# A burst of attention beside a projection: sums over keys first, scores behind them; and sums of exponentials ahead of a subtraction

## The chip, the cores and the metric

The kernel runs on one core of a Trainium2 chip. The metric is the device time of one execution in microseconds. The engines run at the same time and meet through semaphores: TensorE (PE in the profile) multiplies matrices into PSUM, VectorE (DVE) and ScalarE (ACT) work elementwise, GpSimd (POOL) helps with casts, and SyncE (SP) issues most DMAs. PEld is the loading of TensorE's weights.

## The reference

Eight images of 512 channels by 32x32 pixels (1024 tokens) go through two attention layers, in float32.

Layer 0, per image: group norm (32 groups); `qkv = qkv_w @ h + qkv_b`, split into 8 heads of 64 channels; q, k and v are quantized to 256 levels, each with one scale and zero point over the whole tensor; per head `w = softmax(q^T k / sqrt(64))` and `a = w v`; then `x = x + proj_w @ a + proj_b`.

Layer 1, per image: group norm; q, k, v by 512x512 weights; one head of 512 channels: `softmax(q k^T / sqrt(512)) v`; a last 512x512 projection; `x + proj`.

## The kernel before

The quantizer's range needs q, k and v of all images, so a first phase computes these and stores them to DRAM. The second phase takes them up again. Layer 0's attention of the next image runs beside layer 1 of the current one, on the same TensorE, interleaved by Python generators.

**Attention of layer 0** (`attention`, L825). A unit is one pair of heads (j), one half of the 1024 queries (hf) and one block of 128 keys (s), for both heads. A unit's steps:

- `scores`: four st matmuls per two units (64 rows of keys by 512 queries, bf16) into a PSUM tile of two banks. Then ACT takes the exponential into a float32 tile pt. `scores` draws its PSUM tile by `pair_ps` from the pool `ps_s`, which has two buffers (L730).
- `split`: pt is cast to a float16 tile (ACT, or GpSimd for every fourth unit), and VectorE subtracts the cast from pt, so that the two float16 parts carry the value. The pair of parts is the tile two; there are six (L740), and four of pt (L739).
- `over_keys`: av matmuls, the exponentials' parts times v, summed over keys in one PSUM bank.
- `totals`: sm matmuls, the sums of the exponentials over keys, for the division, in another bank.

The loop at L964 makes a burst out of four units: it asks for scores six and eight units ahead, and sums units u to u+3. A burst has two forms: with `dense`, two pairs of units, each av then sm, with the second scores between them; otherwise av of all four, sm of all four, then the second scores. In both, the first scores (units u+6 and u+7) stand at the head of the burst.

**The projection of layer 0** (`project`, L1026). For each half of the tokens and each of four blocks of output channels, four matmuls make one PSUM tile pj of 512 columns (the profile has two rows for each float32 matmul, so 8 of pj for a tile); VectorE evicts it, adding bias and x, and stores it, and takes statistics for layer 1's norm (BN_STATS and an aggregate). Between the two halves it yields, and the attention of the image after gets a burst there. For image 0 the projection's tiles come from the pool `ps_o`. For images 1 to 7 the call at L1482 hands over `score_bank`, so that pj tiles come from the same two buffers of `ps_s` as the scores.

**Layer 1** (`layer1`, L1380). The products are made in seven multiplications instead of eight (`seven`, L1123), with sums of quarters formed on VectorE beforehand. In `o_run` (L1270), exponentials times v, the sums of quarters of the exponentials are t1, t2, t3 and t4. They are made by deferred VectorE operations named "p" to "p4" (L1461 to L1469); "p2" is t2 = p22 - t1. Another deferred kind, "acc" (L1432), adds up the exponentials for the softmax's row sums. Between products 4 and 5 of the second half stands the projection of the next image, with a burst ahead of it, one between its halves, and one behind it (`first`, at L1481 to L1485).

**What sets the order.** Instructions of TensorE, VectorE and ACT run in the order in which the Python program issues them. For VectorE and ACT that order is planned: `InOrder` (L67) keeps a clock for each engine. `later` files an operation with a cost, a time from which it may run and a due time; `fill` picks, up to a limit, the one with the earliest possible start, and at equal starts the earliest due. `settle` forces an operation out before its reader. The bursts are driven at L1622: each yield of the layer's generator advances the attention by one burst, and a negative yield sets `dense` for it.

Of the kernel before, what the change touches and what calls it, by code (L numbers as in the profile page):

```python
# [53 lines left out]
def attn_pair_kernel(  # L54
# [12 lines left out]
    class InOrder:  # L67
# [66 lines left out]
        def settle(self, what):  # L134

            while True:
                i = next((i for i, c in enumerate(self.chores) if c[0] == what), None)
                if i is None:
                    return
                self.begin(i)  # L140

    dve, act, pe = InOrder(nc.vector), InOrder(nc.scalar), InOrder(nc.tensor)
# [137 lines left out]
    with ExitStack() as fast:  # L280
# [544 lines left out]
        def attention():  # L825
# [64 lines left out]
            def over_keys(us):  # L890
                need(us[-1])
                awaits(ready[us[-1]])
                pe.t += 0.12
                for u in us:
                    b, j, hf, s = units[u]
                    if s == 0:
                        avs[b, j, hf] = av_bank(f"av_{b}_{j}_{hf}")
                    for w in range(2):
                        for i, r in enumerate(HALF):
                            mm(  # L900
                                avs[b, j, hf][r, :], lhsT=pairs[b, j][2][:, s, r],
                                rhs=parts[u][:, w, i, :], start=(s == 0 and w == 0),
                                stop=(s == NT - 1 and w == 1),
                            )
# [59 lines left out]
            for u in range(0, len(units), 4):  # L964
                b, j, hf, s = units[u]
                if hf == 0 and s == 0:
                    n = b * PAIRS + j + 1
                    if n < B * PAIRS:
                        pairs[divmod(n, PAIRS)] = load_pair(*divmod(n, PAIRS))
                    settle("qv")  # L970

                def two(what, v):
                    if v < len(units):
                        what(v)
                        what(v + 1)

                pe.t += 0.12  # L980
                two(scores, u + 6)
                if dense:
                    over_keys((u, u + 1))
                    totals((u, u + 1))
                    two(split, u + 6)
                    two(scores, u + 8)
                    over_keys((u + 2, u + 3))
                    totals((u + 2, u + 3))
                else:
                    over_keys(range(u, u + 4))  # L990
                    totals(range(u, u + 4))
                    two(split, u + 6)
                    two(scores, u + 8)
                if s == NT - 4:
                    finish(b, j, hf)
                two(split, u + 8)
                pe.t += 0.15
                last = (j, hf, s) == (PAIRS - 1, NH - 1, NT - 4)
                yield 6.0 + (hf == NH - 1 and s == NT - 4), b + last
# [26 lines left out]
        def project(b, bank=bank):  # L1026

            settle("ao")  # L1030
            st, mvs[b] = stat_tiles(CC, f"b{b}")
            wp0 = wps.pop(b)
            for hf in range(NH):
                for oc in range(CC):
                    ps = bank(f"pj_{b}_{hf}_{oc}")
                    for cc in range(CC):
                        mm(
                            ps, lhsT=wp0[:, cc, bass.ts(oc, P)], rhs=ao[b, cc][:, hf, :],
                            start=(cc == 0), stop=(cc == CC - 1),
                        )  # L1040
                    xx = xts[b][:, oc, bass.ts(hf, 512)]

                    def evict():
                        dve.scalar_tensor_tensor(
                            xx, ps, vec[:, V_PB0 + oc : V_PB0 + oc + 1], xx, ALU.add, ALU.add
                        )
                        nc.sync.dma_start(x1_d[b][oc // 2][hf][:, oc % 2, :], xx)

                    def stats(oc=oc, hf=hf, xx=xx):
                        dve.bn_stats(st[:, oc, hf, :], xx)  # L1050
                        if hf == NH - 1:
                            aggregate(mvs[b], st, oc)

                    dve.do(elements(550), evict)
                    dve.later("pj", 0.62 + 0.2 * hf, stats, within=4.0)
                    chore()
                if hf + 1 < NH:
                    yield -1
            settle("pj")
            for k in [k for k in ao if k[0] == b]:  # L1060
                del ao[k]
# [318 lines left out]
        def layer1(b, steps):  # L1380
# [36 lines left out]
            for hf in range(NH):  # L1417
                last = hf == NH - 1
                if last:
                    gq = yield from a_run(1)  # L1420
                rx = {}
                for row, col in ((0, 0), (1, 1), (1, 0)):
                    load_x1(b, hf, row, col, rx)
                acc = l1p.tile([P, 512], F32, tag="acc1", name=f"acc1_{b}_{hf}")
                pts, rows = {}, []

                def gather(pt, row, acc=acc, rows=rows):
                    for i in range(2):
                        rows.append(pt[:, 2 * row + i, :])
                        if len(rows) > 1:  # L1430
                            two = rows[0] if len(rows) == 2 else acc, rows[-1]
                            dve.later(  # L1432
                                "acc", elements(512), lambda two=two: tt(acc, *two, ALU.add), act.t,
                                7.0,
                            )


                ps_ = [
                    gq[:, i : i + 2].rearrange("p s k n -> p (s k) n") for i in (0, 2, 4)
                ]  # L1440
                t1, t2, t4 = ps_
                for ns in alike:
                    yield from run(
                        *(s_block(b, hf, n, gq, pts, gather) for n in ns),
                        at=3 + 2 * hf - ns[0],
                    )
                    if ns[0] == 0:
                        (p11, p12) = (pts[0][:, :, c * 256 : (c + 1) * 256] for c in range(2))
                        dve.later(
                            "p", elements(1024),  # L1450
                            lambda t1=t1, p11=p11, p12=p12: tt(t1, p12, p11, ALU.subtract),
                            act.t, 12.0,
                        )
                p21, p22 = (pts[1][:, :, c * 256 : (c + 1) * 256] for c in range(2))
                settle("p")

                def third(p12=p12, p22=p22):
                    settle("acc")
                    tt(p12, p22, p12, ALU.subtract)

                dve.later(  # L1461
                    "p2", elements(1024), lambda t1=t1, t2=t2, p22=p22: tt(t2, p22, t1, ALU.subtract),
                    dve.t, 5.0,
                )
                dve.later("p3", elements(1024), third, act.t, 9.0)
                dve.later(
                    "p4", elements(1024), lambda t4=t4, t2=t2, p21=p21: tt(t4, p21, t2, ALU.subtract),
                    act.t, 14.0,
                )  # L1469
                if last and b + 1 < B:  # L1470
                    load_wp(b + 1, act.dma_start)
                    load_x2(b + 1, act.dma_start)
                if done >= B:
                    load_x1(b, hf, 0, 1, rx, aop)
                settle("v")
                between = [lambda: iter((1,)), lambda: iter(()), lambda: iter(())]
                if b + 1 < B and last:

                    def first():
                        nonlocal ahead  # L1480
                        yield -1  # L1481
                        yield from project(b + 1, score_bank)  # L1482
                        yield 1
                        ahead = norm1(b + 1, score_bank)
                        next(ahead)  # L1485

                    def more():
                        next(ahead)
                        yield from ()

                    between = [first, more, more]
                yield from o_run(b, hf, vt, vs, ps_, pts, acc, rx, between)
# [95 lines left out]
        F_FIRST = 12.0  # L1588
        pos, done = 0.0, 0
        dense = True  # L1590

        def advance():
            nonlocal pos, done
# [26 lines left out]
            e.t = pe.t  # L1620
        InOrder.planned = True
        for n in others():  # L1622
            dense = n < 0
            advance()


# [362 lines left out]
```

## Time and profile before

| | us |
|---|---|
| median of 3 runs | 2689.42 (2688.77 to 2689.55) |
| the profiled execution's own time | 2690.02 |
| its span, first to last instruction | 2688.2 |
| PE busy | 2594.8 |
| DVE busy | 1904.8 |
| ACT busy | 1259.0 |
| POOL busy | 201.7 |

The profiled execution took 1.8 us more than its span, and 0.6 us more than the median run. The first phase, and attention of image 0, last until 787 us, where the projection of image 0 begins. From 1031 us a projection begins every 244.7 to 246.4 us: that is one image of layer 1 with the next image's attention inside. The last image's layer 1 (from 2494 us) has no attention beside it.

A row of the timeline gives the start, the time to the end of the merged instructions, the engine, line, operation and tiles, the count, and in brackets the idle time of the engine before it and what ended it. L81 and L192 are the recording helpers, so rows are told apart by their tiles: st are scores, pt exponentials, two the float16 parts, av and sm the sums over keys, pj the projection, h its evicted output, s, o and g layer 1's products. A row of the waits gives the total, the number and the longest.

### The profile page before, as it was taken

Reading aid. Unit: us, or ns where it says so; the run is one execution under the profiler, and the core shown is the slowest. Engines: PE = TensorE matmul, PEld = TensorE weight load, DVE = VectorE, ACT = ScalarE, POOL = GpSimd, SP = SyncE. Lnnn points to the kernel's source line nnn. Section 1 sums busy time; section 2 is a strip of 40 time slices with the busy share of each in tenths; the row PEclk is TensorE's granted clock in tenths of the full one; section 3 lists DMA queues with packets and bytes.
Section 4 is the critical chain, followed back from the end, with each engine's and each line's share of the span. In section 5 each row is a group of like instructions: output and inputs, shape, how many; then the busy total and the mean of one; then the engine's idle time right before and its main releaser. Section 6 shows DMA issues by size and latency. Waiting matters only on the chain.

```text
span 2688.2 us, 33380 instructions
## 1 busy us (share of the span) xinstructions
PE 2594.8 (97%) x13110; PEld 1657.8 (62%) x13110; DVE 1904.8 (71%) x2749; ACT 1259.0 (47%) x1582; POOL 201.7 (8%) x156
## 2 busy tenths in 40 slices
PE   7999999998779999999999999999999999999998
PEld 3455555553225774776577567757765775677687
DVE  6666666647997776876777687678767776876544
ACT  0011111114875665666476556646664765565021
POOL 0000000000220000100100010001001000100000
PEclk9999999998999999999999999999999999999999
DMA  5323223224421123212322321233133223212311
GB/s 196 113 110 125 101 96 117 94 113 146 134 64 40 56 68 118 95 56 94 111 64 71 107 87 56 79 109 94 56 95 110 64 76 103 87 40 69 112 36 37
DMA packets 147464, 241.97 MB, mean 90 GB/s; under 512 B 26592, under 2 KB 92128, under 8 KB 145760
## 3 DMA queue, kind: packets, MB, share of 16 engines
q1 hardware_dynamic: 116448, 181.50, 20.1%
q10 hardware_dynamic: 30848, 58.23, 6.3%
q8 instruction: 105, 1.72, 0.3%
q14 instruction: 63, 0.52, 0.1%
HBM read 152.86 MB, written 86.28 MB: 89 GB/s over the span
## 4 chain that ended last, share of the span: by engine, by line
PE 78%; DVE 9%; issue 7%; DMA 2%; ACT 2%; POOL 1%; SPq 0%; ACTq 0%; DVEq 0%; POOLq 0%
PE s L192 15%; PE o L192 13%; PE qkps L192 10%; PE pj L192 8%; PE av L192 7%; PE v2ps L192 7%; PE g L192 5%; PE vps L192 5%; PE st L192 4%; PE sm L192 4%; DVE two L81 2%; ACT pt L81 1%; DVE sums L81 1%; DVE x L81 1%; DVE h L81 1%
## 5 line engine op out<-in xcount | busy, mean ns | idle before, releaser
L81 DVE TENSOR_TENSOR two<-pt,two 128x1024 f16<-128x1024 f32 x512 | 618.1, 1225 | 165.9 <-POOL two L873 134.7
L81 ACT ACTIVATE pt<-st,esc 128x1024 f32<-128x1024 f32 x512 | 543.5, 1115 | 371.0 <-PE st L192 348.1
L81 ACT CAST two<-pt 128x1024 f16<-128x1024 f32 x364 | 369.5, 1055 | 7.8 <-ACT p L81 5.1
L873 POOL CAST two<-pt 128x1024 f16<-128x1024 f32 x128 | 177.1, 1384 | 1585.5 <-PE sm L192 1376.4
L81 ACT ACTIVATE u<-qkps,qkb 128x512 f32<-128x512 f32 x84 | 57.7, 687 | 476.5 <-PE qkps L192 472.1
L192 PE MATMUL av<-two,v 128*64 128x512 f16 x2048 | 255.3, 387 | 0.6
L192 PE MATMUL s<-g,h 128*128 128x256 f32 x1024 | 234.2, 381 | 0.0
L192 PE MATMUL pj<-ao,wp 128*128 128x512 f32 x512 | 223.9, 595 | 1.5 <-DVE ao L81 1.5
L192 PEld LDWEIGHTS s<-g,h 128*128 128x128 f32 x1024 | 192.9, 190 | 31.8 <-issue 4.3
L192 PE MATMUL st<-q,k 64*128 64x512 bf16 x1024 | 166.5, 386 | 42.3 <-ACT pt L81 35.6
L192 PEld LDWEIGHTS <-v 128*64 128x64 f16 x2048 | 104.1, 110 | 133.1 <-issue 62.0
L192 PE MATMUL s<-g,sums 128*128 128x256 f32 x768 | 178.4, 381 | 0.2 <-DVE p L81 0.2
L192 PE MATMUL o<-p,v 128*128 128x256 f32 x768 | 175.2, 382 | 0.0
L192 PEld LDWEIGHTS pj<-ao,wp 128*128 128x128 f32 x512 | 96.1, 190 | 123.1 <-issue 112.9
L192 PE MATMUL qkps<-x,wqkv 128*128 128x512 f32 x352 | 163.5, 608 | 1.8 <-DVE x L81 1.8
L192 PEld LDWEIGHTS o<-p,v 128*128 128x128 f32 x768 | 144.3, 190 | 25.6 <-issue 6.9
L192 PEld LDWEIGHTS s<-g,sums 128*128 128x128 f32 x768 | 144.7, 190 | 24.2 <-issue 4.6
L192 PE MATMUL qkps<-sums,wa 128*128 128x512 f32 x336 | 153.3, 592 | 0.0
L192 PE MATMUL sm<-two,ones 128*32 128x512 f16 x2048 | 141.6, 386 | 1.3 <-ACT rs L81 1.3
L192 PEld LDWEIGHTS <-k 64*128 64x128 bf16 x1024 | 36.6, 94 | 165.6 <-issue 163.1
L192 PE MATMUL o<-g,vsum 128*128 128x256 f32 x512 | 125.4, 401 | 11.5 <-DVE g L81 11.5
L192 PE MATMUL g<-h,wa 128*128 128x256 f32 x512 | 122.1, 387 | 2.5 <-DVE h L81 2.5
(193 smaller groups left out, 3504.8 us busy)
## 6 DMA issues: line engine op xcount, KB each, us to landing
rs<-rs_d SPq DMA_DIRECT2D x80, 256.0 KB
x<-in_x_dram SPq DMA_DIRECT2D x32, 512.0 KB
raw<-q_d SPq DMA_DIRECT2D x32, 512.0 KB
raw<-k_d SPq DMA_DIRECT2D x32, 512.0 KB
raw<-v_d SPq DMA_DIRECT2D x32, 512.0 KB
x_d<-h SPq DMA_DIRECT2D x64, 256.0 KB
x<-x_d ACTq DMA_DIRECT2D x64, 256.0 KB
out_dram<-x SPq DMA_DIRECT2D x64, 256.0 KB
```

Source lines behind the costliest of these rows:

```text
L81: ins = op(*args, **kw).ins
L192: ins = nc.tensor.matmul(ps, lhsT=lhsT, rhs=rhs, **kw).ins
L873: copy(two[:, 0], pt)
```

## The change

Three edits. A yield may now be -2 or 2, which sets a flag `late` for its burst (-2 is also negative, so `dense` holds as well, but `late` is asked first). A late burst begins with av of two units, then come the first scores, sm of these units, av and sm of the next two, and the second scores at the end. The yield between the projection's halves becomes -2, and the one behind the projection in `first` becomes 2. The deferred operation "p2" gets another earliest time (ACT's clock instead of VectorE's) and another due time (0.5 instead of 5.0 us).

```diff
@@ attention(), the loop over units
                 pe.t += 0.12
-                two(scores, u + 6)
-                if dense:
+                if not late:
+                    two(scores, u + 6)
+                if late:
+                    over_keys((u, u + 1))
+                    two(scores, u + 6)
+                    totals((u, u + 1))
+                    over_keys((u + 2, u + 3))
+                    totals((u + 2, u + 3))
+                    two(split, u + 6)
+                    two(scores, u + 8)
+                elif dense:
                     over_keys((u, u + 1))
                     totals((u, u + 1))
                     two(split, u + 6)
@@ project(), between the halves
                 if hf + 1 < NH:
-                    yield -1
+                    yield -2
@@ layer1(), the deferred t2
                 dve.later(
                     "p2", elements(1024), lambda t1=t1, t2=t2, p22=p22: tt(t2, p22, t1, ALU.subtract),
-                    dve.t, 5.0,
+                    act.t, 0.5,
                 )
@@ layer1(), first()
                         yield from project(b + 1, score_bank)
-                        yield 1
+                        yield 2
                         ahead = norm1(b + 1, score_bank)
@@ the driver
         dense = True
+        late = False
...
         for n in others():
-            dense = n < 0
+            dense, late = n < 0, abs(n) == 2
             advance()
```

## The prediction

> **What bounds the kernel now.** I read the page first: its busy times, its slices and its chain.
>
> ```profile
> span 2688.2 us, 33380 instructions
> PE 2594.8 (97%) x13110; PEld 1657.8 (62%) x13110; DVE 1904.8 (71%) x2749; ACT 1259.0 (47%) x1582; POOL 201.7 (8%) x156
> PE 78%; DVE 9%; issue 7%; DMA 2%; ACT 2%; POOL 1%; SPq 0%; ACTq 0%; DVEq 0%; POOLq 0%
> ```
>
> PE is busy 97% and holds 78% of the chain; every other engine has slack. So a reordering can only gain what PE idles, and it costs whatever PE idles anew. The waits of PE alone, from the first projection that lies beside layer 1 (1031 us) to the end, say how little that is:
>
> ```profile
> PE o L192 <- DVE g L81: 9.6, 5, 1.9
> PE st L192 <- DVE h L81: 6.2, 12, 0.5
> PE st L192 <- ACT pt L81: 1.5, 5, 0.3
> ```
>
> The second line is the one that the change can reach: 12 waits of 0.5 us, two for each of the six projections that take their outputs from the score buffers. Then the timeline of the burst between the halves of one such projection (PE, then ACT), and the head of the burst behind its second half:
>
> ```profile
> 1537.68 0.39 PE L192 MATMUL st<-q,k 64*128 64x512 bf16 x2
> 1538.59 0.39 PE L192 MATMUL st<-q,k 64*128 64x512 bf16 x2 [0.52 <-DVE h L81]
> 1538.91 1.05 PE L192 MATMUL av<-two,v 128*64 128x512 f16 x8
> 1539.90 0.61 PE L192 MATMUL sm<-two,ones 128*32 128x512 f16 x8
> 1540.44 0.61 PE L192 MATMUL st<-q,k 64*128 64x512 bf16 x4
> 1540.98 1.05 PE L192 MATMUL av<-two,v 128*64 128x512 f16 x8
> 1541.96 0.62 PE L192 MATMUL sm<-two,ones 128*32 128x512 f16 x8
> ...
> 1538.11 2.12 ACT L81 ACTIVATE pt<-st,esc 128x1024 f32<-128x1024 f32 x2 [10.46 <-PE st L192]
> 1540.88 2.12 ACT L81 ACTIVATE pt<-st,esc 128x1024 f32<-128x1024 f32 x2 [0.64 <-PE st L192]
> ...
> 1556.44 0.39 PE L192 MATMUL st<-q,k 64*128 64x512 bf16 x2
> 1557.35 0.39 PE L192 MATMUL st<-q,k 64*128 64x512 bf16 x2 [0.52 <-DVE h L81]
> 1557.67 1.92 PE L192 MATMUL av<-two,v 128*64 128x512 f16 x16
> ```
>
> The reader is to see that the second score pair waits for VectorE to evict the last projection tile, that each exponential starts 0.43 to 0.44 us behind its scores, and that 1.53 us of sums (av and sm) stand between the last scores and the next projection tile (1542.51).
>
> Last, stretches of 3.41 us around the long wait of the o products, with the granted clock:
>
> ```profile
> core 0: us, PE busy (x), PEclk, DMA share, GB/s
> 759.15:762.57 3.42, 1.58 (x12) 1.00 0.00 0
> 762.57:765.98 3.41, 2.15 (x16) 0.50 0.00 0
> 1015.15:1018.57 3.42, 1.72 (x8) 1.00 0.74 186
> 1018.57:1021.98 3.41, 3.20 (x15) 1.00 0.01 4
> 1260.91:1264.33 3.42, 1.50 (x7) 1.00 0.35 79
> 1264.33:1267.74 3.41, 3.41 (x10) 0.50 0.00 0
> ```
>
> A stretch with 1.72 us of PE work is followed by full clock, one with 1.58 or less by a stretch at half clock. So idle time of about 1.70 us in a stretch is harmless and 1.83 us halves the next. The stretches keep their own beat: the same wait of 1.9 us halves the clock in images 1, 2, 4 and 5 and not in 0 and 3, where it lies across a boundary. The price shows in the windows from projection to projection: 244.66 us with image 3's, 246.4 us for the others, so 1.7 us.
>
> **The change part by part.** The build's order lists say what moves. ACT, POOL and SP issue the same instructions in the same order, so no DMA is moved. PE runs the same instructions; 13 bursts are reordered: between the halves of projections 0 to 6, and behind projections 1 to 6 (the eighth has no attention left beside it). VectorE has seven swaps beside the projections, and one place where exponential sums move.
>
> *Middle bursts, projections 1 to 6.* Now 1537.68 to 1542.51, 4.83 us. The pieces, start to start: four st matmuls 0.54, eight av 0.985, eight sm 0.55. The new order is av, st, sm, av, sm, st. The first av needs sums that VectorE had ready more than a projection half earlier; the eviction ends 0.86 us behind the burst's start (1538.54), and the second score pair comes at 0.985 + 0.27 = 1.25, so the 0.52 us wait goes. The next scores come at 3.61; the two exponentials before them run 1.42 to 3.54, so that isn't late either. PE's work is 2 x (0.54 + 0.985 + 0.55) = 4.15 us.
>
> But now scores stand last. The projection (score_bank, two buffers) takes its next tile from the buffer that the first of these last scores filled. Its exponential starts at 3.61 + 0.43 = 4.04 and takes 1.11, to 5.15; PE took up work 0.06 us behind an exponential at 805.33. So the projection starts at 5.21: a new wait of 1.06 us, and 0.38 us later than now. Its second tile needs the second exponential (6.16) and comes at 8.6, no wait. Six bursts: +2.3 us. All of PE is queued behind that wait, and VectorE's evictions come 0.38 us later with it. GpSimd's cast of the first pair then starts at the exponential's end (2.53) instead of at the sums' (2.77 now), so it isn't late. ACT ends its exponentials 0.9 us later than now, and the casts behind them; the first subtraction that needs such a cast stands behind an eviction at 8.7, so this is covered by 1.5 us.
>
> *Bursts behind projections 1 to 6.* Now 1556.44 to 1561.04, 4.60 us, av and sm in blocks of 16. New: 4.15 by the same pieces. Behind it come the o products from other buffers, 16 matmuls of 3.7 us, which hide the exponentials; the norm's small matmul, which does use a score buffer, comes after those. Gain 0.45 each, -2.7 us. It reaches the end if the stage behind stays PE's: VectorE finishes the four norm pieces 2.4 us before the g products (1573.55 against 1575.94).
>
> *Middle burst of projection 0.* Its tiles lie in another pool, so nothing waits behind: 802.66 to 807.17 is 4.51, to 4.15: -0.36 us.
>
> *VectorE.* Seven times one subtraction goes behind BN_STATS and the aggregate: 0.69 + 0.21 us later. The eviction behind it still finds all done (the engine idles 0.70 us there), and its reader is a burst more than 10 us on. Cost 0; without cover up to 0.2 us each, since the total is the same. The sums ahead of the subtraction: the lists show it in one place alone, the second half of image 6. Two additions of 0.69 us fill VectorE's 1.29 us idle before 2480.13 and push the subtraction some 0.5 us back, to end near 2481.8; PE reads it at 2486.20. Cost 0; bare, 0.5 us. Everywhere else the wait of 1.9 us before o stays.
>
> *Unseen.* av behind a projection tile, and st behind av, stand nowhere in these bursts; I take the joints at what st behind a projection tile and av behind st cost; between 0 and 0.1 us over 13 bursts, up to +1.3. The shift of all later work by tenths moves the 1.9 us waits against the clock's beat. With -0.36 at image 0 its wait falls whole into a stretch (end 1018.4, boundary 1018.57) and is halved, +1.7; that carries image 1's wait across its boundary, -1.7; the pair repeats at images 3 and 4 or 5. I take four halvings as now, with one more or fewer as bounds: 1.7 either way.
>
> **Sum**: +2.3 - 2.7 - 0.36 = -0.8 us against the profiled execution's own 2690.02 us, which is 0.6 above the median 2689.42. On the median: 2688.6.
>
> Of the idle time, the Trainium skill (Perfetto Trace Analysis, Optimization Strategy) says that a gap which repeats on the saturated engine can mean too few buffers for the next tile. The twelve equal 0.52 us gaps agree, and the rule speaks against this change, which adds no buffer: by it the gap only moves, and the time stays near 2689.4.
>
> Of the clock, TensorE: Matmul & The Clock Gate (Why this matters for your kernels) warns of idle gaps over about 3 us. The rows above halve the clock after 1.8 to 1.9 us, and the measurement decides; by the page's limit no halving would come from any of these waits, and the 1.7 us of doubt would go.
>
> **The rivals.**
> No wait behind the scores: if the projection's tile were free at once, each middle burst gains 0.68 instead of losing 0.38: -4.1 - 2.7 - 0.36 = -7.2, 2682.2 us. For it: no row now shows a projection matmul that waits for an exponential. Against it: now the exponential ends at 1541.99 and the tile starts at 1542.51, a slack of 0.52 us that the new order spends.
> The gain behind the projections is given back (the norm's chain over DMA, VectorE and GpSimd doesn't move with PE): +2.3 - 0.36 = +1.9, 2691.3 us. For it: projection 0 has a 2.5 us wait there. Against: 2.4 us of slack in the others.
> Slower: the projection waits for the second exponential as well, to 6.22. The wait is then 2.07 us, beyond the 1.77 (midway between 1.70 and 1.83) from which the clock halves: 6 x (1.39 + 1.7) - 2.7 - 0.36 = +15.5, 2704.9 us. For it: both tiles of the pair come from one pair of buffers. Against: the scores at 805.33 started as soon as one exponential was done, with the next one running.
> The change doesn't do what it says: for the sums on VectorE that is so at all places but one; priced at 0 above.
>
> **How the numbers follow.** As summed 0.60; one halving more or fewer 0.12 each (2690.3, 2686.9); gain given back 0.07; no wait 0.04; slower 0.05. Some 0.2%, 5.4 us, is what a measurement of this kernel can tell from no change: faster 0.04, same 0.90, slower 0.06, with 0.01 for further waits. The range takes in the halvings, the joints and the gain given back: 2686.2 to 2691.6.
>
> **What would show it.** In the waits of PE after: the line of st behind h gone (6.2 us to about 0), a new line of pj behind pt, some 6 times 1.06 us. The middle bursts 5.2 us long up to the next projection tile, those behind 4.15. The clock at 1.00 behind the new wait; at half in three to five of the six stretches behind the o wait, and not in the same images. Wrong would be a new pj wait near 2 us, a halved clock behind it, or a new wait of g.

## The result and the profile after

The changed kernel took 2687.49 us (median of 20 runs, 2682.78 to 2690.70), the kernel before 2688.77 us over as many runs (2685.17 to 2691.36). The ratio is 0.9996 with a 95% interval of 0.9990 to 1.0003: no change that these runs can tell from none. The profiled execution took 2689.83 us (before: 2690.02), its span 2687.9 us.

The waits of PE from 1031 us to the end, in the changed kernel (total us, number, longest):

```profile
PE o L192 <- DVE g L81: 9.6, 5, 1.9
PE pj L192 <- ACT pt L81: 6.0, 6, 1.0
PE st L192 <- ACT pt L81: 1.5, 5, 0.3
```

The twelve waits of the scores for the eviction (6.2 us) are gone. In their place stand six waits of the projection for an exponential, 6.0 us. The timeline of PE in the changed kernel, with one row of ACT: the middle burst (the one between the projection's halves) and the burst behind the projection, in the same image as in the prediction:

```profile
1536.73 1.05 PE L192 MATMUL av<-two,v 128*64 128x512 f16 x8
1537.72 0.61 PE L192 MATMUL st<-q,k 64*128 64x512 bf16 x4
1538.25 0.61 PE L192 MATMUL sm<-two,ones 128*32 128x512 f16 x8
1538.80 1.05 PE L192 MATMUL av<-two,v 128*64 128x512 f16 x8
1539.78 0.61 PE L192 MATMUL sm<-two,ones 128*32 128x512 f16 x8
1540.33 0.61 PE L192 MATMUL st<-q,k 64*128 64x512 bf16 x4
1541.93 14.00 PE L192 MATMUL pj<-ao,wp 128*128 128x512 f32 x32 [0.99 <-ACT pt L81]
...
1540.76 2.12 ACT L81 ACTIVATE pt<-st,esc 128x1024 f32<-128x1024 f32 x2 [0.49 <-PE st L192]
...
1555.86 1.05 PE L192 MATMUL av<-two,v 128*64 128x512 f16 x8
...
1559.46 0.61 PE L192 MATMUL st<-q,k 64*128 64x512 bf16 x4
1559.99 2.21 PE L192 MATMUL o<-g,vsum 128*128 128x256 f32 x9
```

The first scores (1537.72) stand behind av and wait for nothing. The last scores stand next to the projection, whose first tile comes 0.99 us late: the first of the two exponentials behind these scores starts at 1540.76, takes 1.11 us, and the tile starts 0.06 us behind its end. The middle burst takes 1541.93 - 1536.73 = 5.20 us up to the projection's tile (before 4.83), the burst behind 1559.99 - 1555.86 = 4.13 us (before 4.60). For projection 0 the burst takes 4.13 us (801.38 to 805.51; before 4.51).

The clock, in stretches of 3.41 us of the changed kernel (a stretch with a granted clock of 0.50 is called halved from here on; the wait of o is the 1.9 us wait of layer 1's o products for g):

```profile
core 0: us, PE busy (x), PEclk, DMA share, GB/s
1015.00:1018.41 3.41, 1.50 (x8) 1.00 0.53 115
1018.41:1021.82 3.41, 3.41 (x10) 0.50 0.00 0
1260.76:1264.17 3.41, 1.59 (x8) 1.00 0.77 179
1264.17:1267.58 3.41, 3.31 (x15) 1.00 0.00 0
1540.65:1544.06 3.41, 2.42 (x9) 1.00 0.47 154
1544.06:1547.47 3.41, 3.41 (x9) 1.00 0.06 22
```

Image 0's wait of o is now followed by a halved stretch, and image 1's isn't. Behind the new wait (1540.65, 0.99 us idle) the clock stays full. Of the six stretches behind an o wait four are halved, as before, but in images 0, 2, 3 and 5 instead of 1, 2, 4 and 5.

Where the time went in the two profiled executions, from projection to projection:

| stretch | before, us | after, us |
|---|---|---|
| start to projection 0 (same instructions) | 787.0 | 785.6 |
| projection 0, first to second half | 20.2 | 19.9 |
| to projection 1 | 223.9 | 226.5 |
| projection 1 to 7 | 1462.6 | 1460.9 |
| projection 7 to the end | 194.6 | 195.1 |

The first row differs by 1.4 us although nothing in it was changed; its halved stretches fall differently in the two executions. The third row, +2.6, holds one more halved stretch behind the o wait, and one in the norm of image 0 that moved: before, it began at 834.25 and slowed products that were followed by a wait anyway (g for sums, 2.2 us); after, it began at 840.92, 1.3 us behind the end of that wait, which had grown to 3.7 us. The fourth row, -1.7, holds one halved stretch fewer (-1.7) and the bursts' own gain (0.1 us in each of six images), but one image without a halved stretch took 245.1 us (1769.1 to 2014.2) instead of 244.6, beside a new wait of s for ACT (0.26 us at 1959.77). The last row holds nothing that was moved; it lies between 194.4 and 195.5 us in the nine traces on record.

### The profile page after: what moved, and what is told of

It reads as the page before. It is cut to its first block, busy times and chain, and to the rows that moved or that the text cites. A ratio compares the mean times of both kernels' runs of the same rounds, so it can differ in the third digit from the quotient of the medians.

```text
span 2687.9 us, 33366 instructions
## 1 busy us (share of the span) xinstructions
PE 2596.7 (97%) x13110; PEld 1656.1 (62%) x13110; DVE 1905.7 (71%) x2749; ACT 1259.8 (47%) x1582; POOL 207.0 (8%) x156
## 3 DMA queue, kind: packets, MB, share of 16 engines
q1 hardware_dynamic: 116448, 181.50, 20.2%
## 4 chain that ended last, share of the span: by engine, by line
PE 78%; DVE 9%; issue 7%; ACT 2%; DMA 2%; POOL 1%; ACTq 0%; SPq 0%; DVEq 0%; POOLq 0%
PE s L192 14%; PE o L192 13%; PE qkps L192 10%; PE pj L192 8%; PE av L192 7%; PE v2ps L192 7%; PE g L192 5%; PE vps L192 5%; PE st L192 4%; PE sm L192 4%; DVE two L81 3%; ACT pt L81 1%; DVE sums L81 1%; DVE x L81 1%; DMA out_dram<-x 1%
## 5 line engine op out<-in xcount | busy, mean ns | idle before, releaser
L873 POOL CAST two<-pt 128x1024 f16<-128x1024 f32 x128 | 182.5, 1426 | 1576.9 <-PE sm L192 1174.3
L192 PE MATMUL pj<-ao,wp 128*128 128x512 f32 x512 | 223.9, 595 | 7.5 <-ACT pt L81 6.0
```

The costliest lines, as they stand in the source:

```text
L192: ins = nc.tensor.matmul(ps, lhsT=lhsT, rhs=rhs, **kw).ins
L873: copy(two[:, 0], pt)
```

## The experiments

The theory: each middle burst of projections 1 to 6 trades a wait for an eviction for a longer one for an exponential, each burst behind gains what it lost to the eviction, and the 1.9 us waits decide by their place in a fixed beat whether the clock is halved behind them. The rivals: the gain behind the projection is given back later; the new wait isn't a matter of the order; halved stretches aren't tied to waits of this size.

**The middle burst alone.**

```diff
                         yield from project(b + 1, score_bank)
-                        yield 2
+                        yield 1
```

> The changed kernel with the burst behind the projection put back to its old order; the middle burst and the sums' edit stay. My account (each middle burst of projections 1 to 6 loses 0.38 us to a wait for a score buffer, each burst behind gains 0.45): middle bursts 5.20 us up to the next projection tile, bursts behind 4.60 us, six waits of pj for pt of 1.0 us and six of st for h of 0.5 us, time about 2 us above before (ratio 1.0007). Rival, the gain behind the projection is given back later: the time from one projection to the next stays as in the changed kernel (246.2 to 246.3 us with a halved clock, 244.5 without). Mine: 0.45 us longer, 246.7 and 245.0.

Measured: 2688.79 us, ratio to before 1.0000 (0.9991 to 1.0009); too wide to tell +2 us from nothing. The trace tells it. The waits of PE from 1031 us, in this kernel:

```profile
PE pj L192 <- ACT pt L81: 6.0, 6, 1.0
PE st L192 <- DVE h L81: 3.1, 6, 0.5
```

Six waits of each kind, as expected. From projection to projection, in images without another wait, it takes 245.0 us without a halved stretch (1525.5 to 1770.5; 244.6 in the changed kernel, 1032.0 to 1276.5) and 246.7 with one (1033.3 to 1280.0; 246.3). The 0.46 to 0.47 us that the burst behind gains reaches the next projection; the rival falls.

**The burst behind alone.**

```diff
                 if hf + 1 < NH:
-                    yield -2
+                    yield -1
```

> The changed kernel with the middle burst put back to its old order; the burst behind the projection and the sums' edit stay. My account: no wait of pj for pt, six waits of st for h (middle) of 0.5 us, middle bursts 4.83, bursts behind 4.13 us, 246.4 - 0.45 = 245.9 us from projection to projection with a halved clock and 244.2 without; 2.7 us below before in all (ratio 0.9990). Rival, the gain behind is given back later: 246.4 and 244.7 us, as before.

Measured: 2686.32 us, ratio 0.9991 (0.9982 to 1.0000); -2.4 us. The waits of PE from 1031 us:

```profile
PE o L192 <- DVE g L81: 9.6, 5, 1.9
PE st L192 <- DVE h L81: 3.1, 6, 0.5
PE st L192 <- ACT pt L81: 1.5, 5, 0.3
```

No wait of pj. 245.9 us with a halved stretch (1031.8 to 1277.7), 244.2 without (1521.9 to 1766.1), both as expected to 0.1 us. By the trace this half of the change is a small gain by itself; the interval of the runs just reaches no change.

**The middle burst with scores one unit at a time.**

```diff
                 if late and dense:
+                    one(scores, u + 6)
                     over_keys((u, u + 1))
-                    two(scores, u + 6)
+                    one(scores, u + 7)
                     totals((u, u + 1))
-                    over_keys((u + 2, u + 3))
-                    totals((u + 2, u + 3))
                     two(split, u + 6)
-                    two(scores, u + 8)
+                    one(scores, u + 8)
+                    over_keys((u + 2, u + 3))
+                    one(scores, u + 9)
+                    totals((u + 2, u + 3))
```

> The changed kernel with the middle burst's scores taken one unit at a time: scores, av, scores, sm, scores, av, scores, sm, so that the first scores stand ahead of the sums, where they need only the eviction before last, and sums follow the last scores. My account (the new wait is the exponential behind the last scores, not the order as such): both waits go, the middle burst is 4.15 us, no line of pj behind pt, 246.4 - 0.68 - 0.45 = 245.2 us from projection to projection with a halved clock, 243.5 without; 7 us below before (ratio 0.9973). Rival, the projection's tile waits for more than one exponential, or ACT is late in any order: a wait of pj for pt of 0.5 us or more stays and the middle burst takes over 4.6 us.

Measured: 2684.03 us, ratio 0.9985 (0.9976 to 0.9994): a gain, but less than the 7 us expected (0.9973), which lie outside the interval. The timeline of PE in the same middle burst:

```profile
1532.39 0.39 PE L192 MATMUL st<-q,k 64*128 64x512 bf16 x2
1532.71 1.05 PE L192 MATMUL av<-two,v 128*64 128x512 f16 x8
1533.70 0.39 PE L192 MATMUL st<-q,k 64*128 64x512 bf16 x2
1534.02 0.61 PE L192 MATMUL sm<-two,ones 128*32 128x512 f16 x8
1534.57 0.39 PE L192 MATMUL st<-q,k 64*128 64x512 bf16 x2
1534.89 1.05 PE L192 MATMUL av<-two,v 128*64 128x512 f16 x8
1535.87 0.39 PE L192 MATMUL st<-q,k 64*128 64x512 bf16 x2
1536.19 0.61 PE L192 MATMUL sm<-two,ones 128*32 128x512 f16 x8
1536.74 8.85 PE L192 MATMUL pj<-ao,wp 128*128 128x512 f32 x20
```

No wait stands in it, neither the old nor the new one: the first scores need only the eviction before last, and the exponential that frees the projection's buffer runs beside av and sm. So the new wait was the order's. The burst takes 4.35 us instead of the 4.15 expected: a lone score pair takes 0.32 us start to start, two together 0.54. That is 1.2 us of the missing gain over six bursts. By the trace an image without a halved stretch takes 243.7 us (1029.4 to 1273.1), 0.95 us less than before: 5.7 us in six images, which lies inside the runs' interval of 1.6 to 6.5 us.

**The early subtraction.** In the o products, the subtraction t2 is forced out on VectorE before the burst behind the first product instead of behind the second product.

```diff
                 if step == 1:
+                    settle("p2")
                     yield 1
-                elif step == 2:
-                    settle("p2")
                 elif step == 3:
                     settle("p3")
```

> The changed kernel with the subtraction t2 = p22 - t1 forced out on VectorE before the burst behind the first o product, instead of behind the eviction of the second. It takes away the 1.9 us wait of o for g. My account (a stretch of 3.41 us with 1.82 us or more of idle PE halves the clock of the next, worth 1.7 us each): the six waits of 1.9 us go (11.5 us), and with them the three to five halved stretches behind them (5 to 8.5 us); 17 to 20 us below before (ratio 0.9926 to 0.9937), the time from projection to projection 242.7 us for all images alike. Rival, the halved clock isn't tied to that wait: halved stretches stay somewhere in the images, and the gain is 11.5 us (ratio 0.9957). Second rival, p3 or the row sums become the next wait: a wait of o or sm_l of over 1 us appears, and the gain is below 8 us.

Measured: 2670.10 us, ratio 0.9932 (0.9918 to 0.9945). The waits of PE from 1031 us, and the timeline of PE where the 1.9 us wait of image 5 was:

```profile
PE pj L192 <- ACT pt L81: 6.0, 6, 1.0
PE st L192 <- ACT pt L81: 1.5, 5, 0.3
PE o L192 <- DVE p L81: 0.8, 5, 0.2
```

```profile
2228.16 3.72 PE L192 MATMUL o<-p,v 128*128 128x256 f32 x16
2231.71 3.62 PE L192 MATMUL o<-g,vsum 128*128 128x256 f32 x16
2235.26 0.42 PE L192 MATMUL sm_l<-acc,ones 128*32 128x128 f32 x8
2235.85 3.72 PE L192 MATMUL o<-p,v 128*128 128x256 f32 x16 [0.16 <-DVE p L81]
```

The wait of o for g is gone, and 0.16 us of the next one has come up. No stretch between 850 and 2600 us is halved, and the time from projection to projection is 242.6 us in four of five images (243.2 in the other), by the expectation 242.7. Had only the waits gone and the halved stretches stayed, the ratio would be near 0.9957, outside the interval.

**The new wait doubled.** The exponential behind the first of the last scores of each middle burst is computed twice. All of the computation is kept.

```diff
+                if again:
+                    act.activation(pt, st, AF.Exp, scale=esc)
                 there = act.do(
                     1.12, lambda: act.activation(pt, st, AF.Exp, scale=esc),
...
-                    two(scores, u + 8)
+                    scores(u + 8, again=True)
+                    scores(u + 9)
```

> The changed kernel with the exponential behind the first of the last scores of each middle burst computed twice, one behind the other, into the same tile. Nothing of the computation is left out or altered. My account: it holds the score buffer 1.0 us longer, so the wait of pj for pt is 2.0 us instead of 1.0 in projections 1 to 6, six times 1.0 us in all; and where such a wait lies whole in a stretch of 3.41 us (the traces so far put the limit for full-width products between 1.904 and 1.913 us of idle time) the next stretch runs at half clock, 1.7 us each, in two to four of the six: 9 to 13 us above the changed kernel, some 8 to 12 above before (ratio 1.0030 to 1.0045). Rival, waits below 3 us leave the clock alone: 6 us above the changed kernel and no halved stretch behind a pj wait. Second rival, the projection had a wait on the second exponential in reserve, or VectorE's evictions hide some of it: the wait grows by less than 0.8 us.

Measured: 2707.08 us (2694.37 to 2711.42), ratio 1.0063 (1.0044 to 1.0082): more than expected, 1.0045 at most. The wait grew to 2.14 us, and the clock, in stretches of 3.41 us behind an o wait and behind a pj wait of one image:

```profile
1758.40:1761.81 3.41, 1.50 (x8) 1.00 0.49 111
1761.81:1765.22 3.41, 3.41 (x10) 0.50 0.00 0
1792.53:1795.94 3.41, 1.27 (x13) 1.00 0.40 154
1795.94:1799.35 3.41, 3.41 (x5) 0.50 0.00 0
```

Six of six pj waits and six of six o waits are followed by half clock in the profiled execution. Against the changed kernel that is 6 x 1.15 us of wait, six halved stretches behind pj and two more behind o at 1.7 us each: 20.5 us; from projection 0 to projection 7 the two traces differ by 20.3, and the medians by 19.6. The rival, waits below 3 us leaving the clock alone, would have given some 7. Why all of them were hit and not two to four is told below.

**The sums' edit undone.**

```diff
-                    act.t, 0.5,
+                    dve.t, 5.0,
```

> The changed kernel with the sums' edit undone (t2 = p22 - t1 filed with its old earliest and due times). My account: it moved two additions in one place, the second half of image 6, where TensorE reads t2 4 us later: no wait of PE changes, the time from the seventh projection to the eighth (232.4 us in the changed kernel) stays within 0.1 us. Rival, it took an idle piece off VectorE that is seen at the end: 0.5 us or more there.

One run, 2691.49 us. From the seventh projection to the eighth it is 232.4 us in both kernels (2262.9 to 2495.3; 2260.4 to 2492.8), and no wait of PE for VectorE of over 0.4 us beside the known ones. In this place the edit costs and gives nothing.

**Both gains together.**

The edits of the scores one unit at a time and of the early subtraction.

> The changed kernel with the middle burst's scores taken one unit at a time, and with the subtraction t2 forced out before the burst behind the first o product: the two experiments that gained, together. My account (the two gains lie in different stages and add up): middle bursts 4.35 us, no wait of pj for pt, of st for h or of o for g, no halved stretch between 850 and 2600 us, 241.7 us from projection to projection, 5 us below the kernel with the early subtraction alone, 24 us below before (ratio 0.991). Rival, they share slack on VectorE or ACT: a wait comes back and the gain is below 20 us (ratio over 0.9925).

Measured: 2662.26 us (2661.18 to 2668.60), ratio 0.9912 (0.9898 to 0.9925). All waits of PE from 1031 us:

```profile
PE st L192 <- ACT pt L81: 1.5, 5, 0.3
PE o L192 <- DVE p L81: 0.8, 5, 0.2
PE s L192 <- DVE p L81: 0.2, 1, 0.2
```

Before, this part of the kernel had 17.5 us of waits (9.6 + 6.2 + 1.5 and 0.2 of s) and four halved stretches, 6.8 us; left are 2.5 us of waits and no halved stretch. From projection to projection it takes 241.7 to 241.8 us. This kernel beats both the one before and the changed one.

## Why the prediction was right

*What bounds the kernel.* PE's waits moved, and with them the time. That a reorder can gain only what PE idles is a little too strict: sixteen av in a row take 1.85 us and twice eight 1.97, two lone score pairs 0.64 and two together 0.54. The prediction's pieces, taken start to start, already hold this.

*The middle bursts of projections 1 to 6.* Predicted 5.21 us with a wait of 1.06, measured 5.20 with 0.99 (the profile counts the wait from the end of the last st row, 0.61 us behind its start; the prediction's pieces count 0.54). The step that carried the forecast, that the projection draws from the scores' two buffers and so waits for the exponential behind the last scores, is shown from three sides: with the burst put back the wait is gone, with the exponential doubled it doubles, with sums behind the last scores it vanishes.

*The bursts behind.* Predicted 4.15, measured 4.13; the gain of 0.47 us reaches the next projection, as the two kernels with one burst each show.

*Projection 0.* Predicted 4.15, measured 4.13, and no wait behind it.

*The sums on VectorE.* Priced at 0, measured at 0. The swapped subtractions beside the projection caused no wait either.

*The joints.* Taken at no cost, bound +1.3 us; the bursts came out 0.01 to 0.02 us shorter than their pieces.

*The sum.* 6 x 0.37 - 6 x 0.47 - 0.38 = -1.0 us, predicted -0.8; the medians differ by 1.3, the ratio by 1.1. The bursts' sum lies well inside the run-to-run spread, and only the traces show it: an image without a halved stretch takes 244.58 us, before 244.66. That a measurement can't tell less than 5.4 us from no change was too cautious: over 20 runs each the interval is 0.07% to either side, 1.8 us.

*The clock.* The forecast that image 0's wait would now be halved, image 1's not, and the pair would come again at images 3 and 4 (or 5), with four in all, came out image by image, but that is largely luck. It reckoned with the 0.36 us of projection 0's burst alone; in the two executions the end of image 0's wait moved by 0.78 us (1018.78 to 1018.00), 1.36 us of it before projection 0, where nothing was changed, and part of it back in the norm. The kernel with the sums' edit undone, whose order differs only in image 6, has its halved stretches in images 0, 2, 4 and 5. The kernel with the burst behind alone, with the same wait of o, has them in 0, 1 and 5, the one with the middle burst alone in 1 and 4. So the count moves too, from two to four in these traces, and the doubt of one more or fewer was narrow. Mis-sized was the limit: I put it between 1.70 and 1.83 us of idle time, by a row from the attention of image 0. In the o products it lies higher: in the rows of the changed kernel above, 1.59 us of work (1.82 us of idle time, the limit named ahead of the early subtraction) is followed by full clock. In the kernel with the burst behind alone:

```profile
1260.43:1263.84 3.41, 1.50 (x8) 1.00 0.59 140
1263.84:1267.25 3.41, 3.41 (x9) 0.50 0.00 0
1506.19:1509.60 3.41, 1.51 (x7) 1.00 0.67 162
1509.60:1513.01 3.41, 3.40 (x16) 1.00 0.00 0
```

A stretch with 1.50 us of PE work halves the next, one with 1.51 does not; worked out from the starts and ends of the matmuls in the nine traces here, no stretch of this stage with up to 1.905 us of idle time halves the next, and of those with 1.913 us or more all but one (1.915) do. The limit is at 1.91 us here, just the length of the wait, so it acts only where the wait lies whole in one stretch. In the attention of image 0 idle time alone doesn't decide: 1.30 us of it was followed by a halved stretch (713.63 in the kernel with the middle burst alone), 1.80 us by full clock (649.77 in the changed kernel). What else counts there stays open. The slower rival's point of decision, 1.77, was therefore too low by 0.14; doubling the wait to 2.14 brought that rival about, at 6 x 1.15 + 8 x 1.7 us. Not foreseen was the halved stretch in image 0's norm, which is free where a wait follows it and costs its 1.7 us where one doesn't.

*The two rules weighed.* That repeating gaps can mean too few buffers (the Trainium skill, Perfetto Trace Analysis, Optimization Strategy) fits the change: 6.2 us of waits went and 6.0 came. It isn't the whole story: with the same two buffers, scores one unit at a time left no gap. The limit of about 3 us for idle gaps (TensorE: Matmul & The Clock Gate, Why this matters for your kernels) is too generous here; 1.91 us was enough, where it lay in one stretch.

## What to carry to other kernels

Where two users share a pool of buffers, an order that frees the first user of its wait can hand it to the second: look at which instruction stands next to the border, and ask what frees its buffer. On a saturated TensorE, add to a wait what the clock does behind it; a wait of 1.9 us cost 3.6 us here where the stretch behind it was halved, and taking six such waits away gave 17 us, where the change gave 1. When an effect is smaller than the spread of the runs, measure it from the trace, from one fixed point of the program to the next, and not from the medians.

## What was not expected

The clock's beat goes with much of the spread between executions. The same instructions reach projection 0 between 781.3 and 788.1 us in the nine traces of this study: at 781.3 and 781.6 us with seven halved stretches on the way, at 784.4 to 787.1 with eight or nine, at 788.1 with ten. That isn't all of it, since with eight alone the times are 784.4 to 787.0 us. The runs of the changed kernel span 8 us (2682.78 to 2690.70); that the beat is the reason there too is likely, but only one of them has a trace.

A kernel can lock to the beat. The halved stretches of one trace lie whole multiples of 3.413 us apart (in the kernel before, 1264.33 to 2247.36 us is 288 of them). With the exponential doubled the time from projection to projection became 249.1 us, which is 73 stretches (249.2):

```profile
1028.10:1277.20 249.10, 244.64 (x1400) 0.99 0.26 83
1277.20:1526.30 249.10, 244.63 (x1400) 0.99 0.26 83
1526.30:1775.40 249.10, 244.64 (x1400) 0.99 0.26 83
```

So every image meets the beat at nearly the same place, and where a wait is followed by a halved stretch once, it is so in the images behind it too. This fits six of six. Without any halved stretch an image would take about 244.58 + 1.15 = 245.7 us, by this estimate 72 stretches (245.8), so the place that image 0 happens to meet would hold either way. One of the six runs took 2694.37 us, 12 to 17 us less than the others; that it met the beat at another place is likely, but there is no trace of it.
